# A two-layer post-norm decoder on one core: value products a step later in layer 0, and a rearranged self-attention in layer 1

## The chip, the cores and the metric

The kernel runs on one core of a Trainium2 chip. The metric is the device time of one execution in microseconds; the time before is the median of three runs. A profile is one further execution, recorded by the hardware profiler.

## The reference

The input x is 2 sequences of 1024 tokens of width 256, in fp32; the context is 2 x 64 tokens. Two layers of three blocks each follow, every block with its residual and a layernorm without weights:

```python
x = LN(x + L0_attn(x))         # L0_attn itself returns x + z: 16 heads of 64, softmax(q k^T / 8) v, then w_o
x = LN(x + L0_xattn(x, ctx))   # one head of 256 against 64 context rows, then gelu(out W1 + b1) W2 + b2
x = LN(x + L0_ffn(x))          # 8 experts, all computed: relu(x W1_e + b1_e) W2_e + b2_e,
                               # mixed by gates = entmax_1.5(x Wr + br)
x = LN(x + L1_attn(x))         # 16 heads of 16, softmax(q k^T / 4) v, then W_proj
x = LN(x + L1_xattn(x, ctx, mask))  # 16 heads of 16 against 64 masked context rows
x = LN(x + L1_ffn(x))          # SwiGLU of width 704, activations and weights rounded to int8 steps
```

Nothing is causal: each self-attention is 1024 by 1024 for every head and sequence.

## The kernel before, in words

The 2048 tokens are four groups (g = 0 to 3) of 512. Tiles come from pools with a fixed number of buffers; an instruction that writes a tile waits until the last reader of the buffer's earlier tile is done. PSUM is divided into two "wide" tiles (128 x 1024), three "bank" tiles (128 x 512) and one "acc" tile. The framework inserts the semaphores. Where the code opens `manual_schedule(engines=...)`, the named engines run their instructions in the order in which the code issues them; engines not named are ordered by a scheduler that may move an instruction ahead of others when its inputs are there.

**Layer 0's self-attention** (`l0_attn`, 0 to about 786 us in the profile) is a pipeline of 128 steps n; a step is 128 query rows of one pair of heads. PE, DVE, ACT and POOL are in written order; SP is not named. A step issues `scores(n + 2)` (L297), the row maxima on DVE (L312) and exponentials on ACT (L317), `turn(n + 1)` (two 32 x 32 block transposes on DVE into the tile `blocks`, L342) and `divided(n + 2)` (POOL scales the probabilities, L328). Two steps make one unit m of the value products: `move` (L346 to L363) copies the 16 blocks of a `blocks` tile to their place in a `turned` tile, twelve of them by DMAs of 128 KB from SP's and ACT's queues (L358, L360), two by POOL at once (L362), two by ACT and POOL a step later (`stays`, L367, L368). `mix(m)` (L379) then multiplies `turned` with the values: 32 matmul instructions into acc. `blocks` and `turned` have two buffers each. `others(n)` issues what is due at step n by a table written by hand: projections of the next pair of heads (L252), whose q and k rows are then copied by DMA to the other half of the partitions (q<-q, k<-k on SP, L266), values (L276), the output projection (L396), and weights. In the loop (L494 to L508) the odd steps run `mix((n - 3) // 2)`, the even ones `others(n - 1)`, `others(n)` and `move(n + 1)`. The last `mix`, the output of group 3 (`self.left_over`) and the layernorms of groups 2 and 3 with their transposes (`self.ends`) are run by the next stage.

**Layer 0's cross-attention and its MLP** (786 to 957) has only PE in written order. It walks over the groups: `up` and `down` (L661, residual added by DVE at L665) with the softmax, turn and mix of the next group between them. `self.ends` is run when g is 0. From g = 2 on `some()` issues parts of `entmax(0)` (from L744), an entmax in closed form by sorting, with a square root written as a power on POOL (L791); what is left of it is kept in `self.rest`.

**The MoE** (957 to about 1781) runs 32 steps n (expert, group) and one more; PE, DVE and ACT are in written order. A step's 21 places in `order` issue `hidden` (L917) of step n and `gather` (L965, gated sum by DVE at L974) of step n - 1; `jobs[i]` are run after place i. In step 0 these are the rest of `entmax(0)` (place 0), the transposes and logits of the last group (3 and 6) and the first parts of `begin(0)` (7 to 10). From step 30 on, `normed(g)` and `turned(g)` make the layernorm and transposes of groups 0 and 1; groups 2 and 3 get their layernorm after the last step.

**Layer 1's self-attention** (`l1_attn`, to about 2281). Heads are 16 wide, so q and k are split into a high part (low 12 bits masked off by DVE, L1097) and a remainder (POOL, L1098) and stacked on the partitions by DMAs (`stacks`, L1131), two heads of a stack on either half of the partitions. `project` (L1087) makes them, `values` (L1112) the values. The kernel has 16 steps of 8 units. Softmax needs the row maxima first: `maxima(u)` computes two 128 x 512 scores (L1154) and reduces each on DVE (L1160). `shifts(n)` turns the maxima of a step into a tile `cz` by four small DVE operations (L1169 to L1173), transposes it on PE (L1176) and copies it to `c`. `products` then compute the scores the other way round (L1190), add the shifts by a further matmul (L1197) and take the exponential on ACT (L1203); `mix` (L1217) multiplies by the values. `taken` and `quotient` (L1237) divide; after the last four heads of a group `turned` (L1255), `output` (L1270, L1275, with the layernorm) and `onward` (transposes, L157) finish it. Only PE is in written order. A prologue issues projections, stacks, values and the transposes of groups 2 and 3 (units -26 to -10), then 18 `maxima` in the units -9 to -1, ahead of the first products. In the loop, unit i issues two `maxima` for work nine units on, with `products` between them, then the `mix` of the unit before, then what is due.

**Layer 1's cross-attention** (to about 2392) starts with `queries(0)` (L1506) and runs n = 0 to 18 with PE in written order; then comes the SwiGLU.

Helpers have one line each: L157 transposes a group, L70 and L74 copy a PSUM tile on DVE or ACT, L178 to L183 make the moments of a layernorm (L183 is a power on POOL), L200 scales it.

Of the kernel before, what the change touches and what calls it, by code (L numbers as in the profile page):

```python
# [18 lines left out]
P = 128  # L19
B, S, D = 2, 1024, 256  # L20
T = B * S
NG = 4
# [11 lines left out]
class Decoder:  # L34
# [181 lines left out]
    def l0_attn(self):  # L216
# [5 lines left out]
        with ExitStack() as s:  # L222
# [246 lines left out]
            with self.tc.manual_schedule(engines=engines):  # L469
# [24 lines left out]
                for n in range(steps):  # L494
                    scores(n + 2)
                    for h in range(2):
                        most(n + 2, h)
                        exponentials(n + 2, h)
                    for h in range(2):
                        turn(n + 1, h)  # L500
                    divided(n + 2)
                    if n % 2:
                        stays()
                        mix((n - 3) // 2)
                    else:
                        others(n - 1)
                        others(n)
                        move(n + 1)  # L508
            assert not extra
# [67 lines left out]
    def l0_xattn(self):  # L577
# [5 lines left out]
        with ExitStack() as s:  # L583
# [113 lines left out]
            with self.tc.manual_schedule(engines={mybir.EngineType.PE}):  # L697
# [7 lines left out]
                for g in range(NG):  # L705
# [6 lines left out]
                    if g == 0:  # L712
                        for job in self.ends:
                            job()
# [123 lines left out]
    def l0_ffn(self):  # L838
        nc, t = self.nc, self.t
        HT = GT // 2  # L840
        with ExitStack() as s:
# [157 lines left out]
            with self.tc.manual_schedule(engines=engines):  # L999
                start = [begin(b) for b in range(B)]  # L1000
                mixed = None
                for n in range(len(steps) + 1):
# [4 lines left out]
                    if n == 0:  # L1007
                        jobs[0] = lambda: [None for _ in self.rest]
                        jobs[3], jobs[6] = self.last_group
                        for k in range(7, 11):  # L1010
                            jobs[k] = lambda: next(start[0])
# [4 lines left out]
                    if n >= len(steps) - NG + 2:  # L1016
                        g = n - (len(steps) - NG + 2)
                        if n < len(steps):
                            jobs[5], jobs[17] = (lambda: normed(g)), (lambda: turned(g))
                    a = hidden(*steps[n]) if n < len(steps) else None  # L1020
# [27 lines left out]
                for g in range(2, NG):  # L1048
                    normed(g)
            self.xT, self.turned = nxT, turned  # L1050
# [5 lines left out]

    def l1_attn(self):
        nc, t = self.nc, self.t
        w = self.weight(t["L1_attn_W_qkv"].rearrange("(c p) o -> p c o", p=P), 2, 3 * D)
        wo = self.weight(t["L1_attn_W_proj"].rearrange("(c p) o -> p c o", p=P), 2, D)  # L1060
        with ExitStack() as s:
            pool = lambda n, k: s.enter_context(self.pool(n, k))
            one, qkp, stp, rawp = pool("la1", 1), pool("qk", 1), pool("st", 2), pool("raw", 1)
# [13 lines left out]

            parts = {}

            def project(b, m, name, blk):  # L1080
                lo, bias = (0, R_LQ) if name == "q" else (D, R_LK)
                if blk == 0:
                    parts[name] = [qkp.tile([P, S], F32, tag=name + half, name=name + half) for half in "hl"]
                cols = slice(blk * 512, (blk + 1) * 512)
                ps = self.bank()
                for c in range(2):
                    nc.tensor.matmul(  # L1087
                        ps, lhsT=w[:, c, lo + m * P : lo + (m + 1) * P],
                        rhs=self.xT[2 * b + blk][:, c, :], start=c == 0, stop=c == 1,
                    )  # L1090
                x = self.wp.tile([P, 2 * S], F32, tag="w", name="w")[:, 0:512]
                nc.scalar.activation(
                    x, ps, AF.Identity, bias=self.cols[:, bias + m : bias + m + 1]
                )

                hi, rest = (p[:, cols] for p in parts[name])
                nc.vector.tensor_scalar(hi.bitcast(I32), x.bitcast(I32), -4096, None, ALU.bitwise_and)  # L1097
                nc.gpsimd.tensor_tensor(rest, x, hi, ALU.subtract)  # L1098
# [25 lines left out]
            def stacks(b, jp, name):  # L1124

                st = stack[b, jp, name] = stp.tile([P, S], F32R, tag=name, name=f"{name}st", bufs=4)
                for a in range(2):
                    at = 32 * (jp % 4) + 16 * a
                    by = nc.scalar if a and b == 0 and jp < 2 else nc.sync
                    for i, x in enumerate((0, 1, 0, 1) if name == "q" else (0, 0, 1, 1)):  # L1130
                        by.dma_start(  # L1131
                            st[64 * a + 16 * i : 64 * a + 16 * i + 16, :].bitcast(F32),
                            parts[name][x][at : at + 16, :],
                        )
# [5 lines left out]
            def maxima(u):  # L1140
# [10 lines left out]
                sc = [self.bank(), self.bank()]  # L1151
# [6 lines left out]
                for a in range(2):  # L1158
# [102 lines left out]
            def output(g):  # L1261
# [14 lines left out]
                self.x[g] = self.layernorm(r)  # L1276
# [5 lines left out]
            extra = {-15: [(self.turned, (2,))], -14: [(self.turned, (3,))]}  # L1282
# [3 lines left out]

            last = 8 * len(steps)
            both = [(name, blk) for name in "qk" for blk in range(2)]
            for n, (b, quad, qb) in enumerate(steps):
                first = 8 * n  # L1290
                if qb == 0:
                    for i, (name, blk) in enumerate(both):
                        if quad % 2 == 0:
                            at(first - 26 + i, project, b, quad // 2, name, blk)
                    for i, name in enumerate("qk"):
                        for k in range(2):
                            at(first - 20 + 2 * k + i, stacks, b, 2 * quad + k, name)
                    if quad == 0:
# [5 lines left out]
                if quad == 3:  # L1304
                    g = 2 * b + qb
                    at(first + 10, turned, g)
                    at(first + 11, output, g)
                    at(first + 15, onward, g)
# [5 lines left out]
            with self.tc.manual_schedule(engines={mybir.EngineType.PE}):  # L1314
                for unit in range(-26, -9):
                    others(unit)
                for unit in range(-9, 0):
                    maxima(2 * unit + 18)
                    others(unit)
                    maxima(2 * unit + 19)  # L1320
# [9 lines left out]
                for unit in sorted(extra):  # L1330
                    others(unit)
            self.xT = nxT
# [149 lines left out]
    def l1_xattn(self):  # L1482
# [12 lines left out]
        with ExitStack() as s:  # L1495
# [109 lines left out]
            with self.tc.manual_schedule(engines={mybir.EngineType.PE}):  # L1605
# [3 lines left out]
                for n in range(NT + 3):  # L1609
                    if n % 4 == 1 and n // 4 + 1 < NG:  # L1610
# [182 lines left out]
```

## Time and profile before

| | |
|---|---|
| median of 3 runs | 2489.21 us (2487.06 to 2491.77) |
| the profiled execution's own time | 2493.86 us |
| its span | 2492.0 us |
| PE busy | 2346.6 us |
| DVE, ACT, POOL busy | 1686.2, 1107.1, 909.8 us |
| moved by DMA | 168.79 MB in all, 148.05 of it on queue q1, whose packets take 28.6% of 16 engines' span |
| layer 0: self-attention, cross-attention, MoE | 786, 171, 824 us |
| layer 1: self-attention, cross-attention, SwiGLU | 500, 111, 100 us |

How to read it: times of the stages are positions in the trace, from the span's start. The page gives each engine's busy time, the span in 40 slices with a digit for each engine (tenths of busy time) and the granted clock of PE, and groups of instructions by line. A group reads line, engine, operation, out<-in, shape, count. The table of waits gives for each engine which line waited for which engine's line: total us, times, longest. A line of the timeline is start, length, engine, line, operation, and in brackets how long the engine had been idle and who released it. PEld is PE's loading of weights, beside its matmuls.

### The profile page before, as it was taken

How to read it: one execution, taken by the hardware profiler on the slowest of the kernel's cores; microseconds unless marked ns; L12 is line 12 of the kernel's file. 1: busy time of each engine (PE TensorE's matmuls, PEld its weight loads, DVE VectorE, ACT ScalarE, POOL GpSimd, SP SyncE). 2: the span in 40 equal slices, each digit the busy share in tenths (PEclk: the TensorE clock that was granted, in tenths of full speed). 3: DMA queues.
4: the chain of work that ended last, by engine and by line, in shares of the span. 5: the costliest groups of instructions: out<-in, count | busy, mean ns of one | idle time of the engine just before them, and what ended most of it. 6: DMA issues, size and time to landing. Idle time of an engine off the chain costs nothing. (4 is left out here: it accounts for less than half of the span.)

```text
span 2492.0 us, 37380 instructions
## 1 busy us (share of the span) xinstructions
PE 2346.6 (94%) x14062; PEld 1603.8 (64%) x14065; DVE 1686.2 (68%) x2934; ACT 1107.1 (44%) x1730; POOL 909.8 (37%) x747
## 2 busy tenths in 40 slices
PE   8999999999998989999999999999889999998974
PEld 4455545455555658899999999999734444444742
DVE  5888788887784334555555555546678787985786
ACT  4565565565552212233333333333136555663344
POOL 4666666566566122342343342423201001002412
PEclk9999999999999999999999999999979999999995
DMA  7888788787887001010010010100212222300001
GB/s 166 163 160 165 152 174 169 139 164 153 161 161 165 1 0 41 1 39 26 13 35 30 18 46 1 47 5 1 42 26 35 35 35 35 53 16 1 1 1 34
DMA packets 275668, 168.79 MB, mean 68 GB/s; under 512 B 47560, under 2 KB 262176, under 8 KB 275488
## 3 DMA queue, kind: packets, MB, share of 16 engines
q1 hardware_dynamic: 239072, 148.05, 28.6%
q10 hardware_dynamic: 36416, 18.36, 3.7%
q8 instruction: 111, 1.82, 0.3%
q14 instruction: 69, 0.57, 0.1%
HBM read 34.21 MB, written 2.10 MB: 15 GB/s over the span
## 5 line engine op out<-in xcount | busy, mean ns | idle before, releaser
L312 DVE TENSOR_REDUCE nm<-wide 128x1 f32<-128x1024 f32 x256 | 301.3, 1218 | 121.9 <-PE wide L297 120.2
L1160 DVE TENSOR_REDUCE most<-bank 128x1 f32<-128x512 f32 x512 | 325.6, 683 | 56.4 <-PE bank L1154 48.0
L1203 ACT ACTIVATE w<-wide 128x1024 f32<-128x1024 f32 x256 | 248.3, 1022 | 139.1 <-PE wide L1197 130.5
L379 PE MATMUL acc<-turned,v 128*64 128x256 f32 x2048 | 241.3, 389 | 30.0 <-DMA turned<-blocks 14.7
L297 PE MATMUL wide<-k,q 64*128 64x512 f32 x1024 | 258.4, 619 | 9.0 <-ACT p L317 8.3
L317 ACT ACTIVATE p<-wide,nm 128x1024 f32<-128x1024 f32 x128 | 142.6, 1114 | 238.1 <-DVE nm L312 150.0
L328 POOL TENSOR_SCALAR p<-p,sums 128x1024 f32<-128x1024 f32 x128 | 143.2, 1118 | 276.7 <-DVE sums L325 276.7
L379 PEld LDWEIGHTS acc<-turned,v 128*64 128x64 f32 x2048 | 155.5, 140 | 136.4 <-issue 42.7
L906 ACT ACTIVATE mhT<-mhT,cols 128x256 f32<-128x256 f32 (+1 forms) x256 | 143.1, 607 | 141.5 <-DVE mhT L934 98.2
L817 POOL TENSOR_TENSOR hs<-hs,mhT 128x1024 f32<-128x1024 f32 x31 | 102.2, 3297 | 242.6 <-DVE hs L815 242.6
L917 PE MATMUL unit<-xT,w 128*128 128x256 f32 x768 | 182.4, 380 | 0.0
L974 DVE SCALAR_TENSOR_TENSOR r<-acc,gates,r 128x128 f32<-128x128 f32 x256 | 77.7, 345 | 140.7 <-PE acc L965 140.7
L297 PEld LDWEIGHTS wide<-k,q 64*128 64x128 f32 x1024 | 88.5, 187 | 125.3 <-issue 94.6
L342 DVE STREAM_TRANSPOSE blocks<-p 128x1024 f32<-128x1024 f32 x128 | 157.9, 1234 | 11.1 <-DMA turned<-blocks 4.5
L1154 PE MATMUL bank<-kst,qst 64*128 64x512 f32 x512 | 148.9, 483 | 12.7 <-DVE most L1160 12.1
L183 POOL TENSOR_TENSOR rstd<-ve,nhalf 128x4 f32<-128x4 f32 (+2 forms) x28 | 26.1, 931 | 363.0 <-DVE ve L181 362.6
L342 DVE STREAM_TRANSPOSE blocks<-r 128x1024 f32<-128x1024 f32 x128 | 153.8, 1201 | 0.0
L917 PEld LDWEIGHTS unit<-xT,w 128*128 128x128 f32 x768 | 141.0, 190 | 17.2 <-issue 0.7
L1154 PEld LDWEIGHTS bank<-kst,qst 64*128 64x128 f32 x512 | 70.0, 193 | 122.4 <-DVE most L1160 96.2
L328 POOL TENSOR_SCALAR r<-r,sums 128x1024 f32<-128x1024 f32 x128 | 143.3, 1120 | 0.0
L317 ACT ACTIVATE r<-wide,nm 128x1024 f32<-128x1024 f32 x128 | 141.8, 1108 | 0.3 <-issue 0.2
L1217 PE MATMUL acc<-w,v 128*32 128x512 f32 x1024 | 137.8, 610 | 0.0
(327 smaller groups left out, 4543.2 us busy)
## 6 DMA issues: line engine op xcount, KB each, us to landing
turned<-blocks SPq DMA_DIRECT2D x636, 128.0 KB, 2.8
turned<-blocks ACTq DMA_DIRECT2D x132, 128.0 KB, 3.5
w<-in_L_ffn_W SPq DMA_DIRECT2D x16, 1024.0 KB, 5.4
q<-q SPq DMA_DIRECT2D x64, 128.0 KB, 2.4
k<-k SPq DMA_DIRECT2D x32, 128.0 KB, 3.1
qst<-qh SPq DMA_DIRECT2D x60, 64.0 KB, 2.4
qst<-ql SPq DMA_DIRECT2D x60, 64.0 KB, 2.4
kst<-kh SPq DMA_DIRECT2D x60, 64.0 KB, 2.8
```

The source lines that it names most:

```text
L297: nc.tensor.matmul(sc[h][:, kb, :], lhsT=q[rows, qi, at : at + P], rhs=k[rows, ki, :], start=True, stop=True,)
L312: nc.vector.tensor_reduce(nm, sc, AX.XY, ALU.max, negate=True)
L317: nc.scalar.activation(p, sc.rearrange("p a c -> p (a c)"), AF.Exp, bias=nm, accum_out=sums[:, 0, h : h + 1],)
L328: nc.gpsimd.tensor_scalar(p, p, sums[:, 1, h : h + 1], 1.0, ALU.mult, ALU.mult)
L342: nc.vector.transpose(blocks[m][:, :, h, qt, :], p.rearrange("p (j q) -> p j q", q=32))
L379: nc.tensor.matmul(av[own[h], 0:256].rearrange("p (t i q) -> p i t q", t=2, i=4), lhsT=vals[u][:, kt, own[h]], rhs=p[:, h], start=kt == 0, ...
L906: nc.scalar.activation(hT[:, f, cols], hT[:, f, cols], AF.Relu, bias=self.cols[:, col : col + 1])
L917: nc.tensor.matmul(v[:, m, :], lhsT=up[e][k][:, f : f + P], rhs=self.halves[g][k], start=k in (1, 2, 5) and m == 0, stop=True, skip_group_ ...
L1154: nc.tensor.matmul(sc[a], lhsT=stack[b, jp, "q"][rows, q0 : q0 + P], rhs=stack[b, jp, "k"][rows, kb * 512 : (kb + 1) * 512], start=True, s ...
L1160: nc.vector.tensor_reduce(most[n][:, kb, qt, h : h + 1], sc[a], AX.X, ALU.max, negate=True)
L1203: nc.scalar.activation(slot[:, k, :], ps[k].rearrange("p a q -> p (a q)"), AF.Exp, scale=0.25)
L1217: nc.tensor.matmul(mixed[n][o : o + 32, :], lhsT=vals[b][:, kt, 17 * h : 17 * h + 32], rhs=pT[:, a, :], start=kt == 0, stop=kt == 7, tile_ ...
```

## The change

1. In layer 0's loop the value products and `others` change places: `others` now runs in odd steps, `move(n + 1)` and then `mix(n // 2 - 2)` in even ones; one `mix` follows the loop.
2. `self.ends` (layernorms of groups 2 and 3) is run one at g = 0 and one at g = 1.
3. In the MoE's step 0 the last group's jobs go to places 5 and 8, the rest of the first entmax to place 7, `begin(0)` to 11 to 14.
4. The weights of layer 1's self-attention are loaded three steps before the MoE's end, and its first four projections (sequence 0, heads 0 to 7) are issued at the start of the MoE's last step, into tiles of the pool of x and xT. The layernorms of groups 2 and 3 are no longer made there.
5. In layer 1's self-attention PE, DVE and ACT are now all in written order. The prologue is written out: stacks, then nine units of two `maxima` with one of four `values` or four projections (heads 8 to 15) between; these early maxima use one wide tile and one reduction 128 x 1024 to 2 instead of two. The layernorm is issued in parts (`weigh`: moments; `normed`: scaling), for groups 2 and 3 of the MoE's result in the units 11 to 13 and 19 to 21, and for its own groups 10 to 15 units after a step's start.
6. The end of group 3 (`turned`, `output`, `normed`, `onward`) is run by the cross-attention after it, at n = 0 to 3.

```diff
@@ l0_attn
                     if n % 2:
                         stays()
-                        mix((n - 3) // 2)
-                    else:
                         others(n - 1)
                         others(n)
+                    else:
                         move(n + 1)
+                        mix(n // 2 - 2)
+                mix(steps // 2 - 2)
@@ l0_xattn
-                    if g == 0:
-                        for job in self.ends:
-                            job()
+                    if g < 2:
+                        self.ends[g]()
@@ MoE
-                        jobs[0] = lambda: [None for _ in self.rest]
-                        jobs[3], jobs[6] = self.last_group
-                        for k in range(7, 11):
+                        jobs[5], jobs[8] = self.last_group
+                        jobs[7] = lambda: [None for _ in self.rest]
+                        for k in range(11, 15):
                             jobs[k] = lambda: next(start[0])
...
+                    if n == len(steps) - 3:
+                        self.l1_load()
+                    if n == len(steps):
+                        for name in "kq":
+                            for blk in range(2):
+                                self.l1_project(0, 0, name, blk, nxT[blk])
...
-                for g in range(2, NG):
-                    normed(g)
-            self.xT, self.turned = nxT, turned
+            self.xT, self.turned, self.sums = nxT, turned, accs
@@ l1_attn, maxima(u, early=False)
-                sc = [self.bank(), self.bank()]
+                both = self.wide() if early else None
+                sc = [both[:, a, :] if early else self.bank() for a in range(2)]
...
+                if early:
+                    nc.vector.tensor_reduce(
+                        most[n][:, kb, qt, k : k + 3 : 2], both, AX.X, ALU.max, negate=True
+                    )
-                for a in range(2):
+                for a in range(0 if early else 2):
@@ l1_attn
-                self.x[g] = self.layernorm(r)
+                weigh(g, r)
+            def weigh(g, r=None):
+                r = self.sums[g] if r is None else r
+                sums[g] = r, self.moments(r, range(4))
+            def normed(g):
+                r, moments = sums.pop(g)
+                self.x[g] = self.xp.tile([P, 4, D], F32, tag="x", name="xg")
+                self.scaled(self.x[g], r, range(4), *moments)
...
-            extra = {-15: [(self.turned, (2,))], -14: [(self.turned, (3,))]}
+            extra = {}
+            for g, unit in ((2, 11), (3, 19)):
+                for k, f in enumerate((weigh, normed, self.turned)):
+                    at(unit + k, f, g)
...
-                        if quad % 2 == 0:
+                        if quad % 2 == 0 and n > 4:
                             at(first - 26 + i, project, b, quad // 2, name, blk)
...
-                if quad == 3:
+                if quad == 3 and n < len(steps) - 1:
                     g = 2 * b + qb
-                    at(first + 10, turned, g)
-                    at(first + 11, output, g)
-                    at(first + 15, onward, g)
+                    for k, f in ((10, turned), (11, output), (13, normed), (15, onward)):
+                        at(first + k, f, g)
...
-            with self.tc.manual_schedule(engines={mybir.EngineType.PE}):
-                for unit in range(-26, -9):
+            engines = {mybir.EngineType.PE, mybir.EngineType.DVE, mybir.EngineType.Activation}
+            with self.tc.manual_schedule(engines=engines):
+                for k in range(2):
+                    for name in "kq":
+                        stacks(0, k, name)
+                jobs = [lambda k=k: values(0, k) for k in range(4)]
+                jobs += [lambda a=a: project(0, 1, *a) for a in both]
+                for unit in range(-9, 0):
+                    maxima(2 * unit + 18, True)
+                    maxima(2 * unit + 19, True)
+                    if jobs:
+                        jobs.pop(0)()
                     others(unit)
-                for unit in range(-9, 0):
-                    maxima(2 * unit + 18)
-                    others(unit)
-                    maxima(2 * unit + 19)
...
+            self.ends = [lambda f=f: f(3) for f in (turned, output, normed, onward)]
@@ l1_xattn
                 for n in range(NT + 3):
+                    if n < 4:
+                        self.ends[n]()
```

`l1_project` is the former `project` of `l1_attn` with its weights and tiles taken from the kernel's object; `l1_load` is its load of weights.

## The prediction

> **What bounds the kernel now.** I read the page's busy shares, then its 40 slices, then PE's table of waits, and last the timeline around each wait that the diff touches.
>
> ```profile
> PE 2346.6 (94%) x14062; PEld 1603.8 (64%) x14065; DVE 1686.2 (68%) x2934; ACT 1107.1 (44%) x1730; POOL 909.8 (37%) x747
> PE   8999999999998989999999999999889999998974
> PEclk9999999999999999999999999999979999999995
> ```
>
> PE is busy 94% of the span of 2492.0 us, so at most 145 us of idle PE can be taken out; the change removes almost no PE work. It has to win by closing PE's gaps, and each gap it opens costs its full length. The 8s and the PEclk 7 (slice 29) say where: layer 0's attention (0 to 786), the MoE's ends, the start of layer 1's attention. Next, PE's table of waits (total, times, longest):
>
> ```profile
> PE acc L379 <- DMA turned<-blocks: 14.7, 9, 3.4
> PE bank L1154 <- DVE most L1160: 12.1, 14, 1.8
> PE bank L661 <- DVE r L665: 8.6, 1, 8.6
> PE acc L379 <- DMA q<-q: 6.3, 3, 4.6
> PE bank L157 <- DVE xg L200: 6.0, 3, 3.6
> PE acc L379 <- POOL turned L368: 3.5, 1, 3.5
> ```
>
> The value products (L379) wait 30.0 us in all (their row among the page's groups; these three rows are 24.5 of it), one wait of 8.6 us stands in layer 0's cross-attention, and layer 1's start and end add theirs. The timeline (start, length, engine, line, [idle before <- releaser]) at those places:
>
> ```profile
> 573.88 5.36 PE L379 MATMUL acc<-turned,v 128*64 128x256 f32 x32 [4.60 <-DMA q<-q]
> ...
> 776.72 2.10 POOL L362 COPY turned<-blocks 32x1024 f32<-32x1024 f32 x2
> 779.96 6.54 PE L379 MATMUL acc<-turned,v 128*64 128x256 f32 x32 [3.48 <-POOL turned L368]
> ...
> 903.47 10.55 POOL L791 TENSOR_TENSOR esq<-u,eroot 128x64 f32<-128x64 f32 x1 [0.88 <-DVE u L790]
> 914.05 0.23 DVE L793 TENSOR_TENSOR esq<-emean,esq 128x64 f32<-128x64 f32 x1 [10.33 <-POOL esq L791]
> 917.30 9.65 PE L661 MATMUL bank<-w,xhT 128*128 128x256 f32 x32 [8.64 <-DVE r L665]
> ...
> 1804.91 0.79 PE L1154 MATMUL bank<-kst,qst 64*128 64x512 f32 x1 [0.78 <-DVE most L1160]
> 1914.26 1.28 DVE L1160 TENSOR_REDUCE most<-bank 128x1 f32<-128x512 f32 x2
> 1914.78 0.66 PE L1176 MATMUL bank<-ident,cz 128*128 128x128 f32 x4
> ...
> 2280.94 5.25 PE L1506 MATMUL bank<-xT,lxwqT 128*128 128x512 f32 x8
> ```
>
> **A. Value products one step later.** Two undisturbed steps (303.97 to 314.39) take PE 10.42 us: scores 1.99 twice, mix 3.67, a projection 1.88, values 1.16 (overlapping by some tenths). From 100 to 700 PE is busy 569.16 of 600 us, so the pair averages 10.9. Moving mix(m) from step 2m+3 to 2m+4 gives its copies one step (5.2 us) more than the longest wait of 4.6. It also places move(m+2), which needs the buffer of mix(m), just ahead of mix(m) in the same step. Scores and mix end 1.99 + 3.67 = 5.66 us into the step; the second transpose that the move needs anyway ends 5.9 us after (a step starting at 307.57, move's first copy issued at 313.46). So the new wait is hidden by 0.2 us; without that cover, SP (turned copies, then k, q and weights queued behind them) and the ACT and POOL copies start late. SP has about 0.7 us to spare in a pair: it issues for some 9.7 of 10.42.
> How much of the wait goes? The queues must carry 1.86 MB in 10.42 us, 179 GB/s. The Trainium skill's "DMA: Bandwidth & Descriptors", section "Where 436 GB/s comes from", gives on-chip copies a ceiling of 435 GB/s, by which everything could catch up and all 26.5 us (30.0 less the tail's 3.5) would go. The trace's one-microsecond stretches at a full DMA share move about 205 GB/s. I take the row: the queue runs at 88% of what it can do, and a later step gives slack, not bandwidth. The next limits, q and k rows now projected a step later, and the transposes' two buffers, have 2 to 4 us of play, like the waits. I take two thirds, -18, and +2 for the first mix's later start: **-16** (ends -27 and 0).
>
> **B. Its tail.** The last mix waits 3.48 us for POOL, whose copies at 776.72 stood behind a power of a layernorm (L183, 775.75); afterwards the move stands ahead of it. The wait goes, and the cold 6.54 us falls towards 3.67: -3.5 - 2.9 = **-6.4** (ends -3.5 and -6.4).
>
> **C. Layer 0's cross-attention.** The end of the first group's entmax (L793 on) is now placed behind FFN work, at jobs 5 to 8 instead of 0 to 6. Before, DVE stood 10.33 us behind POOL's 10.55 us power, PE 8.64, and its next 32 matmuls took 9.65 instead of 7.17 (their sum over the group before): -8.6 - 2.5 = -11. The two layernorm ends split between groups 0 and 1 undo waits of 2.4 us and a cold stretch of 1.6: -3, half sure. The 12 small DVE operations now stand in the first FFN step, 3 us of DVE where PE had waited 0.7: +1. Sum **-13** (ends -8 and -15).
>
> **D. Start of layer 1.** Before: the MoE's last matmul ends near 1780.8, then projections, values, transposes, and 36 maxima with 36 reduces, 1800.77 to 1831.1, to the first product at 1834.52. After: four projections (7.4 us of PE) are put ahead of the last gather. They are no less work, so the gather ends near 1784.5; stacks land by about 1785.3. The maxima start then, in 9 units that also take 4 values and 4 projections. A unit's reduces cost DVE two of 1.218 us (L312's row, 1024 wide) = 2.44, instead of four of 0.683. With the job's own DVE work (0.7 for values, 0.3 for the split): 4x3.1 + 4x2.75 + 2.5 = 26. With 3.4 for the shifts as before, products begin at 1785.3 + 26 + 3.4 = 1814.7: **-20**.
> Here the clock matters. The Trainium skill's "TensorE: Matmul & The Clock Gate", "Part 1: The HAM clock gate", halves the clock after an idle window of about 3.4 us. The row disagrees: with no gap above 0.79 in 1801 to 1816 the matmuls took 0.79 instead of 0.50, and the granted clock was 0.59 over 1800 to 1850. By the rule PE (2.8 us a unit with its job) stays under DVE's 3.1 and the 26 holds; by the row, if the clock stays at 0.59, a unit takes 4.7 and the nine 40. As PE is now busy nine tenths of the unit, not half, I take the warm value, ends -12 and -23.
>
> **E. The loop of layer 1.** Plain steps of 8 units take 23.83 us; DVE's four reduces (0.60 to 0.62 each) fill 2.42 of the 2.82 us of a unit. Out go four projections, 4x1.75 = -7.0; in come the transposes of groups 2 and 3, +1.9, and their moments and scalings, 2.4 + 1.4 us of DVE each; of this 7.6 about half is over the 0.4 us a unit that DVE has spare: +4. Layernorms in parts ease later bursts: -1.
> The new wait: DVE and ACT now follow the written order. The four small operations of a shift (0.67 us with their gaps) had been put after the unit's first two reduces (1913.69 to 1914.36), so the transposes at 1914.78 followed PE's mix without delay. Now they stand behind all four: 2 reduces later, 1.25 us, of which some 0.15 is hidden. PE's transposes, then the next unit's maxima and products, and ACT's exponentials wait behind them. 1.1 us at 13 full and 2 partly covered shifts: +15 (bounds 0 and +16; below nothing is excluded, since the order only adds to what DVE must finish first). Sum -7 + 1.9 + 4 - 1 + 15 = **+13** (ends -4 and +20).
>
> **F. End of layer 1's attention.** The last mix ends near 2268.9 and the queries start at 2280.94, behind a chain of output, layernorm and transposes. With the last group's end in the next stage, the queries (of group 0) start about 2270.2: -10.7. The 6.9 us of PE work put in later fills waits there of 2.3 (L1542) and more: +4.7. **-6** (ends -9 and -2).
>
> **Sum.** -16 - 6.4 - 13 - 20 + 13 - 6 = -48.4. Against the profiled execution (2493.9 us, its span of 2492.0 and 1.9 around it) that is 2445.5. That execution lies 4.7 us above the median of 2489.2, so the predicted median is 2489.2 - 48.4, about 2441.
>
> **Rivals.**
> (1) Layer 0 keeps its waits, as move waits for mix and the queues stay full; the change does not do there what it says. For it: 88% DMA load, and waits of irregular place. Against: one step of slack exceeds the longest wait. A = 0: 2457, and with some of C missing up to 2465.
> (2) The shift wait is absorbed. DVE's end of the unit is followed by 0.4 us spare, and ACT idles before most exponentials (0.83 to 0.89). Against: PE has 2.71 of 2.82 us. E = -2: 2426.
> (3) Slower than before, by one mechanism: move's wait for mix in SP's queue. If mix ends later than the transposes by d, SP's 9.7 us of issuing starts d later, q, k and weights behind it too, and once past SP's spare 0.7 us each of 61 pairs loses. The rest of the sum is -32, so it decides from 32 / 61 = 0.53 us a pair (0.6 beyond the bound below). At 1.0 us: 2489 - 32 + 61 = 2518. For it: the cover is only 0.2 us and SP is 93% used. Against: turned copies already wait for the transposes.
> (4) About nothing: half of (3)'s loss, with C and F small.
>
> **Chances.** Forecast 0.57 (own range 2428 to 2452), (1) 0.17, (2) 0.14, (3) 0.08, (4) 0.04. The range that leaves out some 2 in 10 runs from 2421, between (2) and C, D at their better ends, to 2471, (1) with D cold. A measurement of this kernel can tell about 0.2% (5 us) from no change: faster 0.88, same 0.04, slower 0.08.
>
> **What would show it.** A: the L379 waits on DMA fall from 26.5 to under 10, and no new wait of scores (L297) on q rows over 5 us; a pair averages 10.6. B: no POOL wait at the last mix. C: no PE gap over 3 us near 900. D: first products some 20 us after the MoE's last matmul plus 10, PEclk above 0.8 there. E: a wait of about 1.1 us of the shift transposes on DVE, 13 to 15 times. F: the queries within 2 us of the last mix. The prediction is wrong if PE waits in layer 0's loop grow, if the early maxima run cold, or if the shifts do not wait.

## The result, and the profile after

The changed kernel takes 2467.8 us (median of 5 runs, 2464.7 to 2471.9), the kernel before 2488.6 (5 runs): a ratio of 0.9914, interval 0.9901 to 0.9928, or 21 us faster. Forecast were 48 us. Of the two profiled executions that of before lies 5.2 us above its median and that of after 3.1 below, so that their spans differ by 29.1 us: 2492.0 and 2462.9. The accounts by stage below are made of these spans.

The page after the change: busy shares, PE's row and its granted clock.

```profile
PE 2331.8 (95%) x14062; PEld 1580.2 (64%) x14065; DVE 1677.5 (68%) x2916; ACT 1110.8 (45%) x1730; POOL 911.3 (37%) x747
PE   7999999999998999999999999999989999999974
PEclk9999999999999999999999999999999999999986
```

Slice 15 (entmax) and slice 29 (end of the MoE), an 8 before, are full now. Slice 30 (start of layer 1) is still an 8, but the clock's 7 there is gone. Layer 0's slices (1 to 13), which should have gained most, are no fuller. Six rows of PE's waits (line, waited for, total, times, longest):

```profile
PE wide L297 <- ACT p L317: 17.4, 19, 2.9
PE bank L1202 <- DVE cz L1199: 17.0, 15, 3.2
PE bank L1176 <- DVE most L1186: 11.8, 16, 2.1
PE bank L157 <- ACT q L76: 4.7, 2, 2.4
PE bank L396 <- ACT aoT L74: 2.2, 1, 2.2
PE acc L379 <- ACT aoT L74: 1.7, 1, 1.7
```

The value products wait 2.2 us in all instead of 30.0. But the scores (L297) wait 17.4 for ACT's exponentials instead of 8.3, and inside layer 0 the output products and transposes (L396, L157) wait where they had not. The second row is the shift of layer 1, new as forecast. The same places as the prediction showed of before, in the timeline of after:

```profile
781.98 3.67 PE L379 MATMUL acc<-turned,v 128*64 128x256 f32 x32 [0.52 <-POOL rstd L183]
...
1824.52 0.18 DVE L1199 TENSOR_TENSOR cz<-nm,nmh 128x16 f32<-128x16 f32 x1
1824.75 0.66 PE L1202 MATMUL bank<-ident,cz 128*128 128x128 f32 x4 [0.97 <-DVE cz L1199]
...
2250.21 0.66 PE L1263 MATMUL bank<-ident,raw 128*128 128x128 f32 x4 [0.71 <-ACT raw L74]
2250.70 3.60 PE L1552 MATMUL bank<-xT,lxwqT 128*128 128x512 f32 x8
```

The last mix is warm and waits 0.52 instead of 3.48; a shift waits about 1 us; the queries start 2.3 us after the start of layer 1's last mix (2248.44) instead of 13.1. By stage, from the first or last instruction of the named lines (us; A to F are the prediction's parts):

| stretch | before | after | difference | forecast |
|---|---|---|---|---|
| start to last start of L379 (A, B) | 786.1 | 785.3 | -0.8 | -22.4 |
| to the first matmul of the MoE (C) | 170.9 | 156.6 | -14.3 | -13 with the next row's +1 |
| to the MoE's last gather | 823.5 | 829.0 | +5.5 | in C and D |
| to the first product of layer 1 (D) | 54.0 | 28.9 | -25.1 | -20 with the row above |
| to the last product (E) | 430.4 | 445.7 | +15.3 | +13 |
| to the queries (F) | 16.0 | 5.2 | -10.8 | -6 with the next row |
| to the end | 211.1 | 212.2 | +1.1 | in F |

Of the 19.3 us by which the spans miss the forecast, 21.6 are in the first row; the others together are 2.3 better than forecast.

Where did layer 0's waits go? Two rows of the page tell, the value products and the transposes into `blocks`, first before, then after (the last part is the idle time before them):

```profile
L379 PE MATMUL acc<-turned,v 128*64 128x256 f32 x2048 | 241.3, 389 | 30.0 <-DMA turned<-blocks 14.7
L342 DVE STREAM_TRANSPOSE blocks<-p 128x1024 f32<-128x1024 f32 x128 | 157.9, 1234 | 11.1 <-DMA turned<-blocks 4.5
```

```profile
L379 PE MATMUL acc<-turned,v 128*64 128x256 f32 x2048 | 235.1, 382 | 2.2 <-ACT aoT L74 1.7
L342 DVE STREAM_TRANSPOSE blocks<-p 128x1024 f32<-128x1024 f32 x128 | 158.0, 1234 | 43.0 <-DMA turned<-blocks 13.3
```

DVE now stands 43.0 us ahead of the transposes, because the copies out of the `blocks` tile are not done. (The profile names these copies for 13.3 of the 43.0; for 10.2 and 8.5 it names copies of q rows and loads of weights, which use the same semaphores. In the program the DMAs that these transposes wait for are the copies out of `blocks` alone.) DVE works in written order, so the next maxima and with them ACT's exponentials come late, and PE's scores wait for the exponentials to free their PSUM tile. Some groups of eight scores also ran longer than 1.99 us (mostly 2.23; 36 of 128 beyond 2.1, before 8), so the busy time of L297 rose from 258.4 to 271.5. That is the same lateness, in another place.

### The profile page after: what moved, and what is told of

Its sections match the earlier page's. It is cut to its first block, busy times and chain, and to the rows that moved or that the text cites. A ratio compares the mean times of both kernels' runs of the same rounds, so it can differ in the third digit from the quotient of the medians.

```text
span 2462.9 us, 37293 instructions
## 1 busy us (share of the span) xinstructions
PE 2331.8 (95%) x14062; PEld 1580.2 (64%) x14065; DVE 1677.5 (68%) x2916; ACT 1110.8 (45%) x1730; POOL 911.3 (37%) x747
## 5 line engine op out<-in xcount | busy, mean ns | idle before, releaser
L1186 DVE TENSOR_REDUCE most<-bank 128x1 f32<-128x512 f32 x476 | 300.4, 684 | 25.3 <-PE bank L1176 17.3
L297 PE MATMUL wide<-k,q 64*128 64x512 f32 x1024 | 271.5, 627 | 18.8 <-ACT p L317 17.4
L379 PE MATMUL acc<-turned,v 128*64 128x256 f32 x2048 | 235.1, 382 | 2.2 <-ACT aoT L74 1.7
L379 PEld LDWEIGHTS acc<-turned,v 128*64 128x64 f32 x2048 | 142.6, 137 | 113.6 <-issue 30.7
L342 DVE STREAM_TRANSPOSE blocks<-p 128x1024 f32<-128x1024 f32 x128 | 158.0, 1234 | 43.0 <-DMA turned<-blocks 13.3
L297 PEld LDWEIGHTS wide<-k,q 64*128 64x128 f32 x1024 | 89.9, 187 | 146.1 <-issue 76.5
L1243 PE MATMUL acc<-w,v 128*32 128x512 f32 x1024 | 137.2, 608 | 0.0
L1176 PE MATMUL bank<-kst,qst 64*128 64x512 f32 x476 | 125.9, 459 | 11.8 <-DVE most L1186 11.8
L362 POOL COPY turned<-blocks 32x1024 f32<-32x1024 f32 x128 | 132.0, 1031 | 4.0 <-DVE blocks L342 0.3
```

The source lines that it names most:

```text
L297: nc.tensor.matmul(sc[h][:, kb, :], lhsT=q[rows, qi, at : at + P], rhs=k[rows, ki, :], start=True, stop=True,)
L342: nc.vector.transpose(blocks[m][:, :, h, qt, :], p.rearrange("p (j q) -> p j q", q=32))
L362: nc.gpsimd.tensor_copy(b, a)
L379: nc.tensor.matmul(av[own[h], 0:256].rearrange("p (t i q) -> p i t q", t=2, i=4), lhsT=vals[u][:, kt, own[h]], rhs=p[:, h], start=kt == 0, ...
L1186: nc.vector.tensor_reduce(most[n][:, kb, qt, h : h + 1], sc[a], AX.X, ALU.max, negate=True)
L1243: nc.tensor.matmul(mixed[n][o : o + 32, :], lhsT=vals[b][:, kt, 17 * h : 17 * h + 32], rhs=pT[:, a, :], start=kt == 0, stop=kt == 7, tile_ ...
```

## The experiments

Each kernel was timed in five rounds against the kernel before; "layer 0" is the start of the last value product in its profile.

**e1, only the loop of layer 0; e2, all but that.** The edit, in e1 made to the kernel before, in e2 undone in the changed one:

```diff
-                        mix((n - 3) // 2)
-                    else:
                         others(n - 1)
                         others(n)
+                    else:
                         move(n + 1)
+                        mix(n // 2 - 2)
+                mix(steps // 2 - 2)
```

> The kernel before with only the loop of layer 0 changed (others in odd steps; move, then mix, in even ones). Theory (the copies into turned, issued by SP behind q, k and weights, set the pace through the two blocks buffers, so a later mix only shows the same lateness elsewhere): the waits of L379 fall below 5 us, the waits and stretching of the scores L297 and the waits of the transposes L342 grow by as much; 2485 to 2490 us, within 4 us of before. Rival (the forecast's sum: the waits go for good): 2464 to 2469 us.

> The changed kernel with the old loop of layer 0. Theory (parts A and B together brought about 1 us): 2466 to 2472 us, as the changed kernel. Rival (A and B are worth their 22 us and something else lost them): 2486 to 2492 us.

e1: 2497.2 us, ratio 1.0024 (1.0016 to 1.0032), layer 0 785.9; waits of L379 3.0, of L297 19.7, of the transposes 44.6. e2: 2462.9 us, 0.9894 (0.9877 to 0.9911), layer 0 788.4, waits as before the change. The new loop brought nothing. By e1's interval it cost about 6 us, outside what I had expected, and e2 agrees: without the new loop the changed kernel is some 5 us better (0.9894 beside 0.9914). The two profiles of e1 and before differ by only 0.3 us of span, so where those 6 us lie I cannot show.

**e3, SP relieved by leaving work out.** Loads of weights after the first pair of heads and the copies of q and k rows left out; the scores then read half by half instead of head by head.

```diff
-                    each = [(h, i, own[h - i], i, 2 * i) for h in range(2) for i in range(2)]
+                    each = [(h, kb, own[h], 0, kb) for kb in range(2) for h in range(2)]
```

> The changed kernel, but SP carries hardly anything beside the copies into turned in layer 0's loop: the weights of the first pair of heads serve all pairs (their later loads are left out, so the values are those of other heads), and the scores read the q and k rows that the projection left, so the copies q<-q and k<-k are left out. Theory (SP's order): the copies start within 1 us of the transposes instead of 3.2, the transposes' waits on blocks (43 us) and the scores' waits and stretching (17.4 and about 13) fall to a third, 2440 to 2450 us. Rival (the new wait of move for mix on the two turned buffers): the waits stay, 2464 to 2470 us. Second rival (the transfers themselves are the limit): some 10% fewer bytes, a gain of 5 to 10 us.

2502.4 us, 1.0045 (1.0032 to 1.0058), layer 0 822.6. No one had expected this, and it tests neither: the order of the scores was a second change. Both heads' scores now end together, and DVE waits 1.6 us for the first of them in a step. The experiment was badly made; e5 to e7 take its place.

**e4, shifts ahead of the reductions.**

```diff
                 for unit in range(last + 1):
+                    if unit % 8 == 7:
+                        shifts_first(unit // 8 + 1)   # the four small DVE operations of shifts
                     maxima(2 * unit + 18)
```

> The changed kernel with the four small DVE operations of a shift issued ahead of the unit's reductions instead of behind them. Theory (they are late only because they stand behind four reductions in DVE's written order): the waits of L1202 fall from 17.0 us to under 2 and the loop of layer 1 shortens by 13 to 16 us: 2452 to 2455 us. Rival (DVE is then late for the maxima, or ACT takes the place): waits of L1176 on DVE grow and less than half is gained: 2460 to 2466 us.

2461.1 us, 0.9881 (0.9866 to 0.9896): some 8 us better than the changed kernel. The waits of the shift transposes in the loop (13.8 us of the 17.0; the first shift's 3.2 lies ahead of it) are gone, those of the maxima grew from 11.8 to 14.4 and PE's idle time in the loop fell from 28.1 to 17.2:

```profile
PE bank L1176 <- DVE most L1186: 14.4, 15, 2.1
PE wide L1221 <- ACT w L1234: 2.8, 7, 0.5
```

So the wait came from DVE's written order, as the theory said, but in time the gain is the rival's: 8 us, with part of it taken by the waits of the maxima.

**e5, fewer blocks moved; e8, the same with the old loop.** Every copy to the last 32 partitions left out (for that the attention of layer 0 lacks a quarter of its keys), PE's matmuls the same in number, over 96 rows instead of 128. Of the edit only the first line is shown; the bounds of the lists of copies and the rows of the value products change with it.

```diff
-                    for d in range(4) for i in range(4) for r in [(i + d) % 4]
+                    for d in range(4) for i in range(4) for r in [(i + d) % 4] if r < 3
```

> The changed kernel with a quarter of the blocks left out: the copies to the last 32 partitions of turned are not made (of 16 copies of a pair of steps 12 are left, of 12 DMAs 8, of SP's ten 6), and the value products run over 96 of the 128 rows, so the attention of layer 0 lacks a quarter of its keys. PE's instructions and their sizes stay. Theory (the copies set the pace of layer 0's loop): SP needs some 2.6 us less in a pair, the waits of the transposes on blocks (43 us) nearly vanish, layer 0 shortens by 15 to 25 us to 760 to 770: 2443 to 2453 us. Rival (PE, DVE and ACT's chain from scores to maxima to exponentials sets the pace, and the copies only show it): waits move but the stage stays above 780: 2464 to 2470 us.

> The kernel of e5 (a quarter of the blocks and of the keys of layer 0 left out) with the old loop of layer 0: mix a step earlier. Theory (once the copies no longer set the pace, they arrive in time for the early mix as well, so the later mix buys nothing): layer 0 takes 754 to 760 us as in e5, 2432 to 2441 us in all. Rival (the later step is worth its slack wherever the queue has room): the old loop waits at L379 and takes 770 to 780, 2450 to 2460 us.

e5: 2435.2 us, 0.9784 (0.9771 to 0.9798), layer 0 755.5, the transposes' waits 3.6 us. e8: 2436.4 us, 0.9782 (0.9769 to 0.9796), layer 0 757.4. e5 gains more than I had expected; e8 falls where its theory put it. The chain of copies sets the pace of layer 0; with a third of its DMAs gone neither mix is late (waits of L379 1.6 us in e5; in e8 4.8, one wait, for weights of the next stage). But in both SP also no longer stands until one of ACT's copies has landed (2.5 and 1.5 us in all of layer 0, 169 in the changed kernel), so they do not tell the number of copies from the waits between the queues; e16 below does.

**e6, weights from POOL's queue; e7, q and k rows from ACT's.** Same bytes, other queues.

```diff
-                    nc.sync.dma_start(
+                    (nc.sync if u == 0 else nc.gpsimd).dma_start(      # e6, in load
...
-                        nc.sync.dma_start(st[own[1 - h], 1 + k, :], st[own[h], k, :])
+                        nc.scalar.dma_start(st[own[1 - h], 1 + k, :], st[own[h], k, :])   # e7
```

> The changed kernel with the loads of layer 0's weights (after the first pair of heads) issued from POOL's queue instead of SP's; same bytes. Theory (SP's order: its ten copies start 3 us after their data stands): SP is freed of 1.1 us in three of four pairs and the copies start earlier there; 4 to 10 us gained: 2458 to 2464 us. Rival (the transfers themselves): no change, 2465 to 2471 us, or worse by POOL's own delay.

> The changed kernel with the copies q<-q and k<-k issued from ACT's queue right behind the copy out of PSUM that they read; same bytes. Theory (SP's order): SP no longer waits for the projections and starts its ten copies within 1.5 us of the transposes; 6 to 15 us gained: 2453 to 2462 us. Rival (transfers, or ACT's exponentials delayed by some 0.6 us for each issue): no gain or a loss: 2466 to 2480 us.

e6: 2457.8 us, 0.9876 (0.9860 to 0.9892), layer 0 776.6, transposes' waits 29.4. e7: 2488.6 us, 0.9997 (0.9989 to 1.0006), layer 0 813.5, transposes' waits 83.0. With the same bytes in each, who issues them and when matters: less on SP gains 10 us, more on ACT costs 21.

**e9, e4 and e6 together; e10, the same with the old loop.**

> The changed kernel with e4 and e6 together (shifts ahead of the reductions; weights of layer 0 from POOL's queue). Theory: the two stages don't touch, so 8 and 10 us add: 2446 to 2453 us. Rival: part of either was scatter: 2455 to 2460 us.

> e9 with the old loop of layer 0. Theory (part A brings nothing or costs a few us): within 5 us of e9, 2442 to 2454 us. Rival (with SP freed of the weights, the later mix pays): 2458 to 2468 us.

e9: 2455.3 us, 0.9862 (0.9844 to 0.9879), layer 0 782.4. e10: 2445.5 us, 0.9819 (0.9806 to 0.9833), layer 0 770.0. The gains of e4 and e6 did not add in full (13 us of 18; layer 0, the same code in e6 and e9, took 776.6 and 782.4). With the weights off SP the old loop is 10 us the better one, more than the expected 5: the new loop had a cost of its own that I did not know.

**e11, narrow early maxima.**

```diff
-                    maxima(2 * unit + 18, True)
-                    maxima(2 * unit + 19, True)
+                    maxima(2 * unit + 18)
+                    maxima(2 * unit + 19)
```

> The changed kernel with the early maxima in two banks and two reductions each, as in the loop, instead of one wide reduction. Theory (DVE's reductions set the pace of the nine early units, 2.44 us by two wide ones against 2.73 by four): the stretch from the last gather to the first product grows from 28.9 by 3 to 5 us; 2470 to 2474 us. Rival (PE sets it, with a low clock as before the change): it grows by 8 us and more, PEclk under 0.8, or does not grow at all.

2484.9 us, 0.9977 (0.9968 to 0.9987): from gather to first product 41.6 us instead of 28.9. Both expectations miss the reason. The clock was full (1.00) up to 1798, over the first six units, as after the change; it fell only then (0.76 in 1798 to 1805), and one projection took 3.51 us instead of 1.98. A unit took 4.0 us and more from the first on (2.9 in the changed kernel), because maxima, values and projections now share three banks and wait for one another's readers; in this profile:

```profile
1777.80 1.99 PE L1133 MATMUL bank<-w,xT 128*128 128x256 f32 x8
1779.72 0.49 PE L1176 MATMUL bank<-kst,qst 64*128 64x512 f32 x2
1780.73 1.00 PE L1176 MATMUL bank<-kst,qst 64*128 64x512 f32 x2 [0.52 <-DVE v L1138]
1781.84 1.99 PE L1133 MATMUL bank<-w,xT 128*128 128x256 f32 x8
```

So the wide tile is worth some 13 us, and less through its cheaper reduction (2.44 us a unit instead of 2.73) than by leaving the banks to the other work.

**e12 and e13, q and k rows behind the copies of a move**, in the new and in the old loop; SP in written order, projections two steps earlier, otherwise e9 and e10.

```diff
                         move(n + 1)
+                        while behind:
+                            nc.sync.dma_start(*behind.pop(0))
```

> e9 (new loop of layer 0, weights from POOL, early shifts) with SP in written order and the copies of q and k rows issued behind the ten copies of a move instead of ahead of them (projections two steps earlier to make room). Theory (the new loop's cost is that q, k and weights hold SP up after the transposes): SP's copies start within 0.5 us of the transposes instead of 3.1, the transposes' waits on blocks (30 us) fall below 10, layer 0 takes 757 to 767 us instead of 782: 2430 to 2441 us. Rival (move's wait for mix on the two turned buffers holds the copies): the start stays late, layer 0 above 775, 2448 to 2456 us.

> The same with the old loop of layer 0 (mix a step earlier; e10 otherwise). Theory (SP's start sets the pace in both loops): layer 0 falls from 770 to 757 to 765 us, 2432 to 2440 us, within 4 us of e12. Rival (in the old loop the mix a step earlier then waits for the last copies): waits of L379 stay at 15 us or more and the run stays at 2444 to 2448 us, above e12.

e12: 2459.3 us, 0.9884 (0.9867 to 0.9900), layer 0 782.7. e13: 2444.1 us, 0.9824 (0.9809 to 0.9839), layer 0 772.3. From the end of the transposes to SP's first copy it is, over 63 moves, a median of 0.07 us in e13, and still 2.7 in e12 (to the second copy 0.77 and 4.1). The order in SP's queue is not the cost of the new loop. e12's timeline gave the next theory: the mix ends at 308.8, the transposes at 309.5, ACT issues its two copies at 309.67, SP its first at 309.97 and its second only at 313.41.

**e14 and e15, all copies of a move by SP**, in the new and the old loop, otherwise e9 and e10; **e16 and e17, the same one line in the changed kernel and in the kernel before.**

```diff
-                few = 6 if n == steps - 1 else 2
+                few = 6 if n == steps - 1 else 0
```

> e9 (new loop, weights from POOL, early shifts) with all twelve copies of a move issued by SP, none by ACT (but for the last move). Theory (in the new loop SP's copies wait in mid-burst for the landing of ACT's two copies of the same move, 3.4 us after their issue): SP's copies go out without that gap, the transposes' waits on blocks (30 us) fall below 10 although SP issues two copies (1.3 us) more, layer 0 falls from 782 to 765 to 773: 2438 to 2446 us. Rival (the two turned buffers, move's wait for mix): layer 0 stays at 778 or more, 2450 to 2460 us.

> e10 (old loop otherwise as e9) with all twelve copies issued by SP. Theory (SP has waited for ACT's copies there too, but less): layer 0 at 766 to 773 us beside 770, 2441 to 2448 us. Rival (SP's 1.3 us more of issuing sets the pace): 776 and more, 2450 us and more.

> The changed kernel with one line different: all twelve copies of a move by SP, none by ACT (but for the last move); weights, q and k stay in SP's queue. Theory (ACT's two copies hold up SP's in the new loop, and that alone ate the gain of the later mix): layer 0 falls from 785 to 755 to 765 us, 2438 to 2450 us, near the forecast of 2441. Rival (the gain in e14 needs the weights off SP's queue as well): layer 0 at 772 or more, 2455 us or more.

> The kernel before with all twelve copies of a move by SP. Theory (in the old loop ACT's copies cost little, and SP's 1.3 us more of issuing shows as waits of the mix): layer 0 at 786 to 796 us, 2488 to 2500 us. Rival (ACT's copies were the cost there too): 770 us and 2475 us or less.

| | ratio to before (interval) | us | layer 0 |
|---|---|---|---|
| e14, new loop | 0.9761 (0.9747 to 0.9775) | 2431.1 | 755.4 |
| e15, old loop | 0.9839 (0.9824 to 0.9854) | 2450.2 | 776.2 |
| e16, changed kernel | 0.9780 (0.9767 to 0.9793) | 2437.1 | 756.8 |
| e17, kernel before | 0.9985 (0.9978 to 0.9992) | 2486.9 | 777.3 |

With the one line the changed kernel is 31 to 33 us faster (by medians and by ratios), and the later mix is worth 21 us of layer 0 (777.3 to 756.8, and 776.2 to 755.4) and 19 us of time (e15 to e14). e14 and e16 beat both kernels. In the old loop the line does not do this. e15 came out as its rival said, 5 us slower than e10, and e17, some 3 us faster than before, as neither expectation said.

The cause can be seen in SP's waits in layer 0 (first before, then after, then e16):

```profile
SPq L358 <- DMA turned<-blocks: 52.1, 41, 3.2
SPq L237 <- DMA turned<-blocks: 16.8, 10, 3.7
```

```profile
SPq L266 <- DMA turned<-blocks: 71.3, 26, 6.1
SPq L237 <- DMA turned<-blocks: 64.9, 23, 6.2
SPq L358 <- DMA turned<-blocks: 33.0, 20, 5.4
```

```profile
SPq L358 <- DMA turned<-blocks: 4.5, 2, 4.1
```

SP stood 169 us until a copy had landed, before 69, in e16 4.5. One such wait in the changed kernel, with the DMA share of the stretches 97 to 100.3, 100.3 to 101.3 and 101.3 to 103 (the last three numbers of a row are clock, DMA share and GB/s):

```profile
97.26 1.52 ACTq L360 DMA_DIRECT2D turned<-blocks  x2
```

```profile
97.28 0.56 SPq L266 DMA_DIRECT2D q<-q  x1
...
100.69 0.51 SPq L266 DMA_DIRECT2D q<-q  x1
101.24 1.13 SPq L237 DMA_DIRECT2D wk<-in_L_attn_w_k  x2
102.48 0.64 SPq L358 DMA_DIRECT2D turned<-blocks  x1
```

```profile
97.00:100.30 3.30, 3.30 (x12) 1.35 (x11) 2.46 (x5) 1.37 (x2) 2.98 (x3) 1.00 1.01 211
100.30:101.30 1.00, 1.00 (x8) 0.76 (x8) 1.00 (x2) 1.00 (x3) 0.94 (x2) 1.00 0.07 14
```

ACT issues its two copies at 97.26; SP issues one copy of q, then nothing for 2.9 us; the DMA engines run empty (share 0.07); after that SP goes on and reaches the ten copies 5.2 us after ACT's. That ACT's two copies are the cause in the new loop is shown by e14 and e16.

The trace also shows the link. Its DMA records name semaphores: the DMAs of SP and ACT take turns at eight, and in the built program a DMA waits until the last one on its own semaphore has landed, whichever queue issued that. In the case shown SP's second copy of q waits at the semaphore of ACT's first copy, and the second load of weights has that of ACT's second. In the whole of layer 0, 169.0 us of SP's waits (68 of them) end at a semaphore whose last DMA was ACT's; before the change it was 68.5 us (50), and no copy of q or k rows was among them, after it 26 are. In e7, with more DMAs on ACT, it is 220.7 us (104).

In the new loop, layer 0 follows the time at which a move's copies are out. From the end of the transposes until SP has issued its last copy, the median of 63 moves is 12.3 us in e7 (layer 0: 813.5), 11.1 in the changed kernel (785.3), 10.2 in e6 (776.6), 8.7 in e16 (756.8) and 8.1 in e14 (755.4). In the old loop it does not (9.8 before with 786.1, 9.9 in e17 with 777.3), and there SP's waits alone are not the cost either: in e13 117 us of them are for ACT's copies, yet the transposes wait 3.6 us in all. Why the old loop bears them better is open.

The 1.3 us that ACT spends on issuing also falls away in e14 and e16; e5, where ACT still issues two copies a move and layer 0 takes 755.5 us, speaks against it as the cause, but no run separates it from the wait at equal bytes.

```profile
L379 PE MATMUL acc<-turned,v 128*64 128x256 f32 x2048 | 235.7, 383 | 0.9 <-POOL rstd L183 0.5
L342 DVE STREAM_TRANSPOSE blocks<-p 128x1024 f32<-128x1024 f32 x128 | 158.0, 1234 | 4.2 <-POOL p L328 3.6
```

These two rows are e16's, beside the 2.2 and 43.0 of the changed kernel: neither the mix nor the transposes wait any more.

## Why the prediction was wrong, point by point

- **The view of the whole** (gaps of PE are what can be won): half right. PE's gaps fell by 14 us, but its busy time fell by 15. The parts B to D name cold stretches; the view of the whole counted on gaps alone.
- **A, value products later, -16: wrong.** The stage with A and B gained 0.8, less than the 2 to 3 us by which layer 0 differs between profiles of the same code. The step that failed is "I take two thirds, -18". It counted the waits of the mix and judged by their length that a step of slack removes them. They were a sign of the copies' pace: the slack went into DVE's waits on `blocks` (11.1 to 43.0 us). I had named the two `blocks` buffers as the next limit and given them 2 to 4 us of play; and I had looked for the price of the new order at move's wait for the mix, hidden by 0.2 us. In the move of e12 told above that cover held (mix 308.8, transposes 309.5). What I did not see is the third thing that the move carries, ACT's two copies, and that SP's DMAs wait for them at shared semaphores: 169 us in the changed kernel, 69 before. With them on SP the same step is worth 21 us (e16 against e17), close to the 22 of A and B together: the slack was worth what I had said, but in another kernel, in which SP's copies do not wait for ACT's.
- **Bytes or fabric.** I weighed the 435 GB/s that the Trainium skill gives ("DMA: Bandwidth & Descriptors", section "Where 436 GB/s comes from") against 205 in the trace and took the row. e16 moves all the bytes in 757 us, at 167 GB/s over 50 to 750 us instead of 161: bandwidth was not what held the copies, neither by the rule nor by the row. My 88% (179 of 205 GB/s) was an average with holes in it, and the holes were the finding.
- **Rival (1)**, layer 0 keeps its waits, at 2457 to 2465: the nearest. Its reason, full queues, was not the one. Rival (3), slower by SP's queue, had the right place, SP behind the move, but not the reason (move's wait for mix). What ACT's copies cost the changed kernel, 28.5 us of layer 0 (785.3 to 756.8 in e16), is 0.47 us a pair, just under the 0.53 from which (3) would have decided.
- **B, -6.4.** The last mix waits 0.52 and is warm: 5.8 less. But in front of it the stage had lost as much, so it is not seen in the time.
- **C, -13:** right in size; -14.3, less the small operations now in the MoE.
- **D, -20:** right in size (MoE's start to first product, 877.5 to 857.9: -19.6). The clock stayed full (1.00 in 1778 to 1798), so the warm value was the right choice. The reason was half right: DVE paces the units only because the wide tile leaves the three banks free (e11).
- **E, +13:** right in mechanism, and +15.3 in this profile; the shift's wait was 17.0 us at 15 places (forecast 15 at 15). Other profiles of the same loop give up to +21 (last section). e4 removed 13.8 of the wait but gained only 8 us of time.
- **F, -6:** -9.7. The queries come 10.8 us sooner, as forecast (10.7), but the work put later costs 1.1 us there instead of 4.7; why is open.

Five of six parts, then, came out near their size, and the sum failed by one term.

## What to carry to other kernels

When a consumer waits for a pipeline of copies, first measure from the data's readiness to the first copy, and look for holes in the DMA share; giving the consumer more slack here only moved the wait to whoever fills the buffers next, until the copies themselves came earlier. Two queues that share the bookkeeping of their DMAs can hold each other up: a change of order of work is also a change of which transfer waits for which. If a late start is the cause, try all copies of a group from one queue before anything larger, and time it: here the same line gained 31 us in one order of the loop, and gained 3 or lost 5 in the other.

## What was not expected of the hardware

- In the new loop two copies of 128 KB issued by ACT beside ten by SP cost the group more than they spared. SP alone issues twelve in 7.9 us without a gap (301.69 to 309.56 in e14); beside ACT's two it stood 2.9 us in the case shown.
- The 96 copies of q and k rows moved from SP to ACT (e7) cost 21 us, though they carry the same bytes.
- The scatter of layer 1's loop: the same instructions took 445.7 and 451.1 us in two kernels that differ only in layer 0 (changed kernel and e2); the mean of L1243 was 608 and 616 ns, the clock 0.99 and 0.98. Over nine profiles with the late shifts it took 445.2 to 451.1, over seven with the early shifts of e4 441.1 to 445.3, and in the old arrangement 430.0 to 430.4 in three. Differences below 5 us in one profile were not read as effects.
